# Attention on one core: VectorE empties the second pair of banks, in plain order; and three smaller moves

## The chip, the cores and the metric

The kernel runs on 1 core of one Trainium2 chip. The metric is device time in microseconds (us) of one execution; the time given is the median of several runs. Engine names: PE is TensorE (PEld its weight loads), DVE is VectorE, ACT is ScalarE, POOL is GpSimd, SP is SyncE, which here only issues DMAs.

## What is computed

Four images x of 64 x 64 positions and 256 channels, a self-attention block with a residual:

```python
B, W, H, C = x.shape          # 4, 64, 64, 256
N = W * H                     # 4096
q = jnp.einsum('bwhc,cd->bwhd', x, Wq) + bq      # C2 = 128 channels
k = jnp.einsum('bwhc,cd->bwhd', x, Wk) + bk
v = jnp.einsum('bwhc,cd->bwhd', x, Wv) + bv      # 256 channels
pq = q.reshape(B, -1, N); pk = k.reshape(B, -1, N); pv = v.reshape(B, -1, N)
energy = jnp.einsum('bcn,bcm->bnm', pq, pk)
attention = jax.nn.softmax(energy, axis=-1)
out = jnp.einsum('bcm,bnm->bcn', pv, attention)
return gamma * out.reshape(B, W, H, C) + x
```

All is float32.

## The kernel before

**Products in three parts.** PE multiplies in a reduced form of float32, so every operand is split into a high part h, a low part l and a combination d, and a product is the sum of three: h with h, l with l, d with d, scaled. Each 128x1024 tile that enters a product so costs one ScalarE pass for h (`upper`, L380) and two VectorE passes for l and d (`halves`, L405 and L407).

**Image 0** is projected first, in 16 units i (NI = 16). A unit transposes a piece of x, splits it (`x_forms`: ScalarE h, VectorE l, POOL d), multiplies it with the weights for q and k together (`products(..., 0, ...)`) and for v (`products(..., 1, ...)`), and splits the results again: `qk_forms` into a tile `f`, from which `store` sends k to DRAM (kf) and q to DRAM (qd) with SP's queue; `v_forms` straight into `vall`. Three tiles `f` take turns. In units 0 to 13 POOL makes the d of v, in the last two VectorE makes both (L164). The PSUM banks of these products come from two rings: the transposes take p0 and p1 in turn (ring 0), the q/k and v products a0, b0, a1, b1 in turn (ring 1). Between the units stand the loads of q (`load_q(0, 0, j)`, a quarter at units 1 to 4), the loads of k (`load_k`, units 2, 4, 6, 8, 11), all on POOL's queue, and the first attention work: `cross` and `energy` of steps 0 and 1, `upper` and `halves(0)`.

**Attention** is 512 steps n, 128 to an image. Eight groups of 16 steps (t = 0 to 15, NU = 16) to an image; a group is 512 query positions, a step 256 key positions. In step n the program does, in this order:

- `cross(n + 2)`: two products d of the energy, each in its own bank, then ScalarE scales the bank in place (L357).
- `attend(n, 0)`: six products of the exponentials with v, for the first 128 output channels; h and l go to bank a0, d to b0, summed over the 16 steps of the group.
- `energy(n + 2)`: four more products into the energy banks, then ScalarE's exponential (L374).
- `upper(n + 2)`: ScalarE's h of them; at t = 0 also `upper(n + 1)`, put off from the step before.
- `step(p, ...)`: a piece of the projection of the next image, spread over the steps.
- `halves(n + 1)`: VectorE adds the exponentials to the running sum (L391), then l (L405) and d (L407).
- `attend(n, 1)`: the same six products for the other 128 channels, banks a1 and b1.

All is written in program order, and each engine takes its instructions in that order; no scheduler changes it.

**At a group's end** the four banks are emptied into a tile `o` by `emptied`, scaled by gam2 and gam1: ScalarE, a pass of 128x512 for each bank (L442). a0 and b0 at t = 15; a1 and b1 in the first step of the next group (images 0 to 2, after `energy`), or in its step t = 1 (image 3, which the code calls `late`). In image 3 the second pair of every other group lies in p0 and p1 instead of a1 and b1, so there the emptying is not urgent. In images 0 to 2 it is: `attend(n, 1)` of t = 0 writes the same banks. The program therefore puts products of the next step in front of it, and takes them out of that step:

```python
            if t == 1 and n > 1 and not late:
                attend(n, 0, (2,))
...
            if t == 0 and n and not late:
                attend(n + 1, 0, (0, 1))
            attend(n, 1)
```

`sums` then adds up the softmax sums on PE (z, L466), and `finish` divides, adds x and stores, in pieces over the following steps.

Of the kernel before, what the change touches and what calls it, by code (L numbers as in the profile page):

```python
# [9 lines left out]
F32 = mybir.dt.float32  # L10
F32R = mybir.dt.float32r
I32 = mybir.dt.int32
AF = mybir.ActivationFunctionType
ALU = mybir.AluOpType
# [6 lines left out]
def kernel(  # L21
# [36 lines left out]
    nc = tc.nc  # L58
    B, W, H, C = x.shape
    P = 128  # L60
# [4 lines left out]
    NI = NM // 2  # L65
# [17 lines left out]
    NJ = NB // P  # L83
    NG = N // NB
# [16 lines left out]
    with ExitStack() as fast:  # L101
# [85 lines left out]
        def bank(name, shape, b, ring):  # L187
            if b:
                tile_ = spare(name, shape)
                now["turn"] += 1  # L190
                return tile_
            pool, tag = next(rings[ring])
            return pool.tile(shape, F32, tag=tag, name=name)
# [45 lines left out]
        def products(b, i, w, fs):  # L239

            xf = units["xf", b, i]
            if fs[0] == 2:
                units[w, b, i] = bank(f"qv{w}_{b}_{i}", [P, 2, C], b, 1)
            to = units[w, b, i]
            for s in range(2):
                for f in fs:
                    for k in range(KC):
                        if w:
                            left, right = wf[:, 1, f, k, s * P : (s + 1) * P], xf[f][:, k]
                        else:  # L250
                            left, right = xf[f][:, k, s, :], wf[:, 0, f, k]
                        nc.tensor.matmul(  # L252
                            to[:, s, :],
                            left,
                            right.rearrange("p s a -> p (s a)") if w else right,
                            start=(f == 2 and s == k == 0),
                            stop=(f == 1 and k == KC - 1),
                            skip_group_check=True,
                        )
# [35 lines left out]
        def qk_forms(b, i):  # L295
            y = units.pop((0, b, i)).rearrange("p s (w a) -> p s w a", w=2)
            if b == 0 and i % 3 == 2:
                f = f3
            else:
                f = work.tile([P, 2, 2, 3, P], F32R, tag="pf", name=f"f_{b}_{i}")  # L300
            h = f[:, :, :, 0, :]
            nc.scalar.activation(h, y, AF.Identity, scale=UPPER / 64)  # L302
            yield
            for j, s, op in ((1, -64.0, ALU.add), (2, 64.0 * (1.0 + E), ALU.subtract)):
                nc.vector.scalar_tensor_tensor(  # L305
                    f[:, :, :, j, :], h.bitcast(F32), s, y, ALU.mult, op
                )
                yield
            for s in range(2):
                stores.append((kf[b, i // 2 + NU // 2 * s][:, i % 2], f[:, s, 1]))  # L310
                stores.append((qd[b, i // NJ + NG // 2 * s][:, i % NJ], f[:, s, 0]))

        def v_forms(i):
            y = units.pop((1, 0, i))
# [9 lines left out]

        def store():
            for to, f in stores:
                nc.sync.dma_start(to, f.bitcast(F32))
            stores.clear()

        def load_v(b, t):  # L330
            for i in range(2):
                nc.gpsimd.dma_start(vall[:, t, i], vf[b, t][:, i])

        def load_q(b, g, j=None):
            loads["q", b, g] = qs[g % 2]
            j = slice(NJ) if j is None else j
            nc.gpsimd.dma_start(loads["q", b, g][:, j], qd[b, g][:, j])

        def load_k(n):
            b, u = divmod(n, STEPS)  # L340
            if b < B:
                t = kpool.tile([P, 2, 3, P], F32R, tag="k", name=f"k_{b}_{u}")
                nc.gpsimd.dma_start(t, kf[b, u % NU])  # L343
                loads["k", n] = t
# [89 lines left out]
                        skip_group_check=True,  # L434
                    )

        def emptied(n, j, banks=None):

            if j == 0:
                now["o"] = work.tile([P, 2, 2, NB], F32, tag="o", name=f"o_{n // NU}", bufs=1)  # L440
            for c, scale in enumerate((gam2, gam1)):
                nc.scalar.activation(  # L442
                    now["o"][:, c, j, :],
                    banks[c] if banks else now["ab"[c], j],
                    AF.Identity,
                    scale=scale,
                )

        def sum_forms(n):

# [163 lines left out]
        rings = cycle(now["banks"]), cycle([(ps_o, tag) for tag in ("a0", "b0", "a1", "b1")])  # L614
        image(0)
        qs = [work.tile([P, NJ, 3, P], F32R, tag=f"q{g}", name=f"q{g}", bufs=1) for g in range(2)]
        f3 = qs[1].rearrange("p (s w) f a -> p s w f a", s=2)
        for i in range(4):
            load_x(0, i)
# [27 lines left out]
        for i in range(NI):  # L647
            products(0, i, 0, (0, 1))
            qk = qk_forms(0, i)
            next(qk)  # L650
            if i == 0:
                products(0, 0, 1, (2,))
                seed_v(0)
                transposed(0, 2)
                load_x(0, 5)
                x2 = x_forms(0, 2)
                next(x2)
                next(x2)
            if i + 1 < NI:
                products(0, i + 1, 0, (2,))  # L660
                seed_qk(0, i + 1)
            next(qk)
            next(qk)
            next(qk, None)
            products(0, i, 1, (0, 1))
            vs = v_forms(i)
            next(vs)
            next(vs)
            next(vs, None)
            if i + 1 < NI:  # L670
                products(0, i + 1, 1, (2,))
                seed_v(i + 1)
            if i + 3 < NI:
                transposed(0, i + 3)
                for _ in x_forms(0, i + 3):
                    pass
            load_x(0, i + 6)
            store()
            if i in (7, 10):
                cross(i // 9)  # L680
            elif i in (8, 11):
                energy(i // 9)
            elif i in (9, 12):
                upper(i // 10)
            elif i == 14:
                halves(0)
            if 1 <= i <= NJ:
                load_q(0, 0, i - 1)
            if i in (2, 4, 6):
                load_k(i // 2 - 1)  # L690
            elif i in (8, 11):
                load_k(3 + i // 9)
        for n in range(B * STEPS):
            b, u = divmod(n, STEPS)
            g, t = divmod(u, NU)
            final = n == B * STEPS - 1
            if n == 0:
                image(1)
                load_x(1, 0)
            if u == STEPS - 5 and b + 2 < B:  # L700
                image(b + 2)
            if n == B * STEPS - 6:
                xr = ppool.tile([P, 2, NB], F32, tag="s", name="xr")
                nc.sync.dma_start(xr, xg[b, g])
            cross(n + LOOK)
            turn = t == NU - 1 and not final
            if t == 0 and n:
                upper(n + LOOK - 1)
            if turn:
                zf = sum_forms(n)  # L710
                next(zf)
            p = n - 3 + (n > 6) + (n > 17)
            step(p, "act")
            late = n >= (B - 1) * STEPS
            if t == 1 and n > 1 and not late:
                attend(n, 0, (2,))
            elif not final:
                attend(n, 0)
            energy(n + LOOK)
            load_k(n + LOOK + 3)  # L720
            store()
            if t == 0 and n:
                done = full
            if t == late and n > 1:
                emptied(n - 1 - late, 1, done)
            if turn:
                emptied(n, 0)
            else:
                upper(n + LOOK)
            step(p, "pe")  # L730
            if t == 2 * late and n > 2:
                sums(n - 1 - 2 * late)
                active.append(finish(n // NU - 1, now["o"], now["total"]))
            halves(n + 1)
            if turn:
                next(zf)
            step(p, "dve")
            if final:
                finish_last(n, xr)
                break  # L740
            if t == 0 and n and not late:
                attend(n + 1, 0, (0, 1))
            attend(n, 1)
            full = now["a", 1], now["b", 1]
            if n in (6, 17):
                for engine in ("act", "pe", "dve"):
                    step(p + 1, engine)
            if t == 6 and n + NU < B * STEPS:
                load_q(*divmod(n // NU + 1, NG))
            if n >= STEPS - NU + 3 and (n - 3) // NU % NG == NG - 1 and (n - 3) // STEPS + 1 < B:  # L750
                load_v((n - 3) // STEPS + 1, (n - 3) % NU)
            proceed()

    NB = 512
    NG = N // NB
# [214 lines left out]
```

## Time and profile before

| | us |
|---|---|
| median of 3 runs | 2358.7 (2357.61 to 2360.9) |
| profiled execution | 2356.93 |
| its span, first to last instruction | 2354.9 |
| PE busy | 2340.9 (99%) |
| VectorE busy | 2126.2 (90%) |
| ScalarE busy | 1852.4 (79%) |
| POOL busy | 416.8 (18%) |

The granted TensorE clock is 0.999 of full speed over the span. The profiled execution is 1.8 us shorter than the median of the runs. In the rows of a timeline the first number is the start in us from the span's beginning, the second how long the row lasts; rows of several instructions are merged (x4). The end of a matmul is modelled, and matmuls overlap, so from one start to the next is what counts. The bracket at the end of a row is the idle time of the engine ahead of it and what ended it. In a list of waits the columns are: engine, what waited, what it waited for, us in total, how many times, the longest.

### The profile page before, as it was taken

What the parts mean: (1) busy time and instruction counts of PE and PEld (TensorE: products, weight loads), DVE (VectorE), ACT (ScalarE), POOL (GpSimd) and SP (SyncE); (2) the same over time, 40 slices, a digit from 0 to 9 for tenths busy, and PEclk for the clock granted to TensorE, in tenths of its full rate; (3) what the DMA queues carried; (4) which work ended last, traced back from release to release, by engine and by line L of the source; (5) the groups of instructions that cost most, each with busy time, mean ns of one, the idle gap of its engine ahead of it and who ended that gap; (6) DMA issues with size and microseconds to landing.
All of it is one profiled execution on the core that took longest, in us unless ns stands there. A gap on an engine that the chain in (4) does not pass through costs nothing.

```text
span 2354.9 us, 31737 instructions
## 1 busy us (share of the span) xinstructions
PE 2340.9 (99%) x10820; PEld 1937.3 (82%) x10820; DVE 2126.2 (90%) x2098; ACT 1852.4 (79%) x3026; POOL 416.8 (18%) x716
## 2 busy tenths in 40 slices
PE   9999999999999999999999999999999999999998
PEld 9888888888888888888888888888888888888887
DVE  7998999999999989999899998999989888888888
ACT  7778777787777877778777788777887777788875
POOL 7111111111321111111131111111113111111110
PEclk9999999999999999999999999999999999999999
DMA  8555665566974666545697555655569644444443
GB/s 284 152 171 164 183 172 150 155 171 182 295 243 149 177 175 172 163 145 169 182 323 229 142 178 168 186 158 150 167 178 339 172 134 123 123 130 112 133 133 96
DMA packets 192650, 413.68 MB, mean 176 GB/s; under 512 B 27585, under 2 KB 78019, under 8 KB 192482
## 3 DMA queue, kind: packets, MB, share of 16 engines
q0 software_dynamic: 101120, 280.54, 44.0%
q1 hardware_dynamic: 90814, 130.77, 15.9%
q8 instruction: 89, 1.46, 0.3%
q14 instruction: 79, 0.65, 0.1%
q10 hardware_dynamic: 548, 0.26, 0.0%
HBM read 306.51 MB, written 104.98 MB: 175 GB/s over the span
## 4 chain that ended last, share of the span: by engine, by line
PE 95%; ACT 2%; DVE 1%; issue 1%; POOL 1%; DMA 0%; DVEq 0%; POOLq 0%; ACTq 0%
PE a L428 39%; PE e L371 20%; PE b L428 19%; PE e L356 10%; PE qv L252 4%; PE v L269 3%; PE xt L218 1%; ACT o L442 1%; ACT x L374 1%; PE z L466 1%; ACT e L357 0%; DMA xs<-in_x_dram 0%; DVE ld L405 0%; ACT h L380 0%; POOL v L160 0%
## 5 line engine op out<-in xcount | busy, mean ns | idle before, releaser
L374 ACT ACTIVATE x<-e 128x512 f32<-128x512 f32 x960 | 522.0, 596 | 299.7 <-PE e L371 299.6
L405 DVE TENSOR_TENSOR ld<-x,h 128x1024 fp32r<-128x1024 f32 x480 | 585.9, 1221 | 94.0 <-ACT h L380 48.7
L391 DVE TENSOR_TENSOR s<-s,x 128x1024 f32<-128x1024 f32 x480 | 586.2, 1221 | 87.1 <-ACT x L374 84.5
L357 ACT ACTIVATE e<-e 128x512 f32<-128x512 f32 x1024 | 547.1, 573 | 138.1 <-PE e L356 138.1
L428 PE MATMUL a<-ld,v 128*128 128x512 f32 x2048 | 634.1, 391 | 1.0
L428 PE MATMUL a<-h,v 128*128 128x512 f32 x2048 | 634.2, 391 | 0.0
L428 PE MATMUL b<-ld,v 128*128 128x512 f32 x2048 | 631.2, 389 | 0.6 <-DVE ld L407 0.5
L343 POOL DMA_DIRECT2D k<-kf x512 | 272.4, 532 | 1890.4 <-PE e L371 1754.9
L407 DVE SCALAR_TENSOR_TENSOR ld<-h,x 128x1024 fp32r<-128x1024 f32 x480 | 584.7, 1218 | 0.0
L371 PE MATMUL e<-q,k 128*128 128x512 f32 x2048 | 552.3, 391 | 1.1
L380 ACT ACTIVATE h<-x 128x1024 fp32r<-128x1024 f32 x480 | 511.0, 1065 | 13.2
L371 PEld LDWEIGHTS e<-q,k 128*128 128x128 f32 x2048 | 379.4, 188 | 94.8 <-ACT e L357 19.9
L428 PEld LDWEIGHTS a<-ld,v 128*128 128x128 f32 x2048 | 382.5, 188 | 90.2 <-DVE ld L405 11.1
L428 PEld LDWEIGHTS b<-ld,v 128*128 128x128 f32 x2048 | 384.1, 188 | 82.3 <-issue 1.1
L428 PEld LDWEIGHTS a<-h,v 128*128 128x128 f32 x2048 | 379.6, 188 | 75.1
L356 PE MATMUL e<-q,k 128*128 128x512 f32 x1024 | 315.6, 389 | 0.0
L356 PEld LDWEIGHTS e<-q,k 128*128 128x128 f32 x1024 | 191.9, 188 | 40.2
L305 DVE SCALAR_TENSOR_TENSOR f<-f,qv 128x512 fp32r<-128x512 f32 x118 | 79.2, 679 | 2.5 <-ACT f L302 2.2
L252 PE MATMUL qv<-wf,xf 128*128 128x256 f32 x576 | 77.5, 285 | 1.7 <-POOL xf L160 1.2
L252 PEld LDWEIGHTS qv<-wf,xf 128*128 128x128 f32 x576 | 73.8, 191 | 5.0 <-POOL xf L160 1.8
L164 DVE SCALAR_TENSOR_TENSOR vf<-vf,v 128x512 fp32r<-128x512 f32 x96 | 65.3, 680 | 0.0
L405 DVE TENSOR_TENSOR ld<-s,h 128x1024 fp32r<-128x1024 f32 x32 | 39.2, 1226 | 28.7 <-ACT h L380 27.3
(91 smaller groups left out, 1163.5 us busy)
## 6 DMA issues: line engine op xcount, KB each, us to landing
k<-kf POOLq DMA_DIRECT2D x512, 384.0 KB, 3.4
vf<-vf SPq DMA_DIRECT2D x96, 384.0 KB
v<-vf POOLq DMA_DIRECT2D x96, 384.0 KB, 6.6
q<-qd POOLq DMA_DIRECT2D x31, 768.0 KB, 4.9
kf<-f SPq DMA_DIRECT2D x118, 192.0 KB
qd<-f SPq DMA_DIRECT2D x118, 192.0 KB
o<-in_x_dram POOLq DMA_DIRECT2D x31, 512.0 KB, 7.0
out_dram<-o SPq DMA_DIRECT2D x31, 512.0 KB
```

The lines of the kernel that those rows point to most:

```text
L252: nc.tensor.matmul(to[:, s, :], left, right.rearrange("p s a -> p (s a)") if w else right, start=(f == 2 and s == k == 0), stop=(f == 1 an ...
L305: nc.vector.scalar_tensor_tensor(f[:, :, :, j, :], h.bitcast(F32), s, y, ALU.mult, op)
L343: nc.gpsimd.dma_start(t, kf[b, u % NU])
L356: nc.tensor.matmul(e, *forms(n, i, 2), start=True, stop=False, skip_group_check=True)
L357: nc.scalar.mul(e, e, -REST)
L371: nc.tensor.matmul(e, *forms(n, i, f), start=False, stop=(f == 1), skip_group_check=True)
L374: nc.scalar.activation(x[:, i, :], e, AF.Exp, scale=(1.0 + E) ** 3 / E)
L380: nc.scalar.activation(h, units[n], AF.Identity, scale=UPPER)
L391: nc.vector.tensor_tensor(s, s, x, ALU.add)
L405: nc.vector.tensor_tensor(l, x, h.bitcast(F32), ALU.subtract)
L407: nc.vector.scalar_tensor_tensor(d, h.bitcast(F32), 1.0 + E, x, ALU.mult, ALU.subtract)
L428: nc.tensor.matmul(to, vall[:, t, i, f, j * P : (j + 1) * P], units[n][f][:, i, :], start=(t == 0 and i == 0 and f != 1), stop=(t == NU - ...
```

## The change

Four edits:

- **Second pair by VectorE.** In images 0 to 2 the banks a1 and b1 are emptied by VectorE (`tensor_scalar`), at t = 0 after the projection's piece for PE and `sums`, ahead of `halves(n + 1)`. The order of the attention products is plain again: `attend(n, 0)` whole in every step, nothing pulled ahead.
- **Last image.** ScalarE empties one bank of the second pair at t = 1 and one at t = 2, each ahead of `energy`.
- **First q copied in SBUF.** The four quarters of the first group's q go from `f` straight to the SBUF tile of q, with POOL's queue, and are not stored to DRAM and loaded again. The loads of k stand at units 3, 6, 9, 11, 13.
- **Last v forms put off.** In units 14 and 15 the v products lie in p0 and p1 instead of b0 and b1, and VectorE's l and d of them come later: those of unit 14 after the q/k forms of unit 15, those of unit 15 after `halves(1)` in step 0.

```diff
             if fs[0] == 2:
-                units[w, b, i] = bank(f"qv{w}_{b}_{i}", [P, 2, C], b, 1)
+                ring = 1
+                if b == 0 and w and i >= NI - 2:
+                    ring = 0
+                    next(rings[1])
+                units[w, b, i] = bank(f"qv{w}_{b}_{i}", [P, 2, C], b, ring)
...
                 stores.append((kf[b, i // 2 + NU // 2 * s][:, i % 2], f[:, s, 1]))
-                stores.append((qd[b, i // NJ + NG // 2 * s][:, i % NJ], f[:, s, 0]))
+                if b or s or i >= NJ:
+                    stores.append((qd[b, i // NJ + NG // 2 * s][:, i % NJ], f[:, s, 0]))
+                else:
+                    stores.append((loads["q", 0, 0][:, i], f[:, s, 0]))
...
             for to, f in stores:
-                nc.sync.dma_start(to, f.bitcast(F32))
+                if to.dtype == F32R:
+                    nc.gpsimd.dma_start(to, f)
+                else:
+                    nc.sync.dma_start(to, f.bitcast(F32))
...
-        def emptied(n, j, banks=None):
+        def emptied(n, j, banks=None, only=None, vector=False):
...
             for c, scale in enumerate((gam2, gam1)):
-                nc.scalar.activation(
-                    now["o"][:, c, j, :],
-                    banks[c] if banks else now["ab"[c], j],
-                    AF.Identity,
-                    scale=scale,
-                )
+                if only in (None, c):
+                    y = banks[c] if banks else now["ab"[c], j]
+                    to = now["o"][:, c, j, :]
+                    if vector:
+                        nc.vector.tensor_scalar(to, y, scale, None, ALU.mult)
+                    else:
+                        nc.scalar.activation(to, y, AF.Identity, scale=scale)
...
             next(qk, None)
+            if i == NI - 1:
+                next(vs)
+                next(vs, None)
             products(0, i, 1, (0, 1))
             vs = v_forms(i)
             next(vs)
-            next(vs)
-            next(vs, None)
+            if i < NI - 2:
+                next(vs)
+                next(vs, None)
...
-            if 1 <= i <= NJ:
-                load_q(0, 0, i - 1)
-            if i in (2, 4, 6):
-                load_k(i // 2 - 1)
-            elif i in (8, 11):
-                load_k(3 + i // 9)
+            if i in (3, 6, 9):
+                load_k(i // 3 - 1)
+            elif i in (11, 13):
+                load_k(i // 2 - 2)
...
-            if t == 1 and n > 1 and not late:
-                attend(n, 0, (2,))
-            elif not final:
+            if not final:
                 attend(n, 0)
+            if late and 1 <= t <= 2 and n > 1:
+                emptied(n - 1 - t, 1, done, t - 1)
             energy(n + LOOK)
...
-            if t == late and n > 1:
-                emptied(n - 1 - late, 1, done)
...
+            if t == 0 and n and not late:
+                emptied(n - 1, 1, done, vector=True)
             halves(n + 1)
+            if n == 0:
+                next(vs)
+                next(vs, None)
...
-            if t == 0 and n and not late:
-                attend(n + 1, 0, (0, 1))
             attend(n, 1)
```

More of the change, by code (lines that the diff above doesn't have):

```diff
@@ L332, in load_v, with load_q @@
                 nc.gpsimd.dma_start(vall[:, t, i], vf[b, t][:, i])
-        def load_q(b, g, j=None):
+        def load_q(b, g):
             loads["q", b, g] = qs[g % 2]
-            j = slice(NJ) if j is None else j
-            nc.gpsimd.dma_start(loads["q", b, g][:, j], qd[b, g][:, j])
+            nc.gpsimd.dma_start(loads["q", b, g], qd[b, g])
         def load_k(n):
@@ L616 @@
         qs = [work.tile([P, NJ, 3, P], F32R, tag=f"q{g}", name=f"q{g}", bufs=1) for g in range(2)]
+        loads["q", 0, 0] = qs[0]
         f3 = qs[1].rearrange("p (s w) f a -> p s w f a", s=2)
```

## Prediction

> **What bounds the kernel now.** I read the page first, then the waits of the weight loads, then the timeline of one group boundary engine by engine. The page says that TensorE (PE) has no room:
>
> ```profile
> span 2354.9 us, 31737 instructions
> ## 1 busy us (share of the span) xinstructions
> PE 2340.9 (99%) x10820; PEld 1937.3 (82%) x10820; DVE 2126.2 (90%) x2098; ACT 1852.4 (79%) x3026; POOL 416.8 (18%) x716
> ```
>
> By the matmul row the most that any reordering can win is 2354.9 - 2340.9 = 14.0 us. But matmul ends are modelled, so a matmul that starts late is hidden under the stretched end of the one before. The weight loads show it:
>
> ```profile
> PEld e L371 <- ACT e L357: 19.9, 62, 0.6
> PEld a L428 <- DVE ld L405: 11.1, 23, 0.5
> PEld qv L252 <- POOL xf L160: 1.8, 2, 1.4
> ```
>
> [...]
>
> The counts give the places away. 23 is the number of group boundaries whose new group lies in the first three images (24 groups, less the start). 62 is twice 31, that is 23 and the 8 boundaries of the last image. So two waits come back at each boundary of images 0 to 2 and one at each of image 3. One such boundary (step 160 has t = 0, step 161 t = 1), on PE:
>
> ```profile
> 798.97 0.63 PE L428 MATMUL a<-h,v 128*128 128x512 f32 x2
> 799.65 0.73 PE L428 MATMUL a<-ld,v 128*128 128x512 f32 x2
> 800.22 0.62 PE L428 MATMUL a<-h,v 128*128 128x512 f32 x2
> 800.68 0.62 PE L428 MATMUL a<-ld,v 128*128 128x512 f32 x2
> 801.14 0.62 PE L428 MATMUL b<-ld,v 128*128 128x512 f32 x2
> 801.59 0.61 PE L356 MATMUL e<-q,k 128*128 128x512 f32 x2
> 802.05 0.61 PE L428 MATMUL b<-ld,v 128*128 128x512 f32 x2
> 802.65 1.22 PE L371 MATMUL e<-q,k 128*128 128x512 f32 x4
> 803.71 1.03 PE L218 MATMUL xt<-ident,x 128*128 128x128 f32 x8
> ```
>
> Starts are what counts. An undisturbed pair takes 0.46 us (800.22 to 801.14 is two pairs). The first two rows are the pulled-forward products `attend(161, 0, (0, 1))`: from h to l takes 0.68, and l itself 0.57, so 0.22 + 0.11 = 0.33 us are lost on l(161), VectorE's L405. The pair left over for t = 1 (802.05) takes 0.60 and the four energy products 1.06 instead of 0.92: 0.14 + 0.14 = 0.28 us lost, on ScalarE's pass L357 over the energy bank, because only two products stand between `cross` and `energy`. Together 0.61 us a boundary.
>
> **Part 1: second pair emptied by VectorE, plain order.** Both places where PE waits come from the order that the change removes. Is there room for two more VectorE passes? VectorE and ScalarE at the same boundary:
>
> ```profile
> 795.16 0.68 DVE L164 SCALAR_TENSOR_TENSOR vf<-vf,v 128x512 fp32r<-128x512 f32 x1
> 795.76 1.22 DVE L391 TENSOR_TENSOR s<-s,x 128x1024 f32<-128x1024 f32 x1
> 798.37 1.22 DVE L405 TENSOR_TENSOR ld<-x,h 128x1024 fp32r<-128x1024 f32 x1 [1.39 <-ACT h L380]
> 799.51 1.22 DVE L407 SCALAR_TENSOR_TENSOR ld<-h,x 128x1024 fp32r<-128x1024 f32 x1
> ```
>
> ```profile
> 796.26 1.10 ACT L357 ACTIVATE e<-e 128x512 f32<-128x512 f32 x2
> ...
> 799.20 0.69 ACT L442 ACTIVATE o<-a,gam 128x512 f32<-128x512 f32 x1
> 799.77 0.70 ACT L442 ACTIVATE o<-b,gam 128x512 f32<-128x512 f32 x1
> 800.34 1.08 ACT L380 ACTIVATE h<-x 128x1024 fp32r<-128x1024 f32 x1
> 801.29 0.56 ACT L467 COPY s<-z 1x512 f32<-1x512 f32 x1
> 802.02 1.07 ACT L357 ACTIVATE e<-e 128x512 f32<-128x512 f32 x2 [0.17 <-PE e L356]
> ```
>
> The trace has no VectorE pass that reads only PSUM. The nearest is L305, one full bank and one SBUF operand:
>
> ```profile
> L305 DVE SCALAR_TENSOR_TENSOR f<-f,qv 128x512 fp32r<-128x512 f32 x118 | 79.2, 679 | 2.5 <-ACT f L302 2.2
> ```
>
> Rows of that size start 0.60 us apart (795.16 to 795.76), so I take 1.2 us for the pair; ScalarE's own 0.70 each, 1.4 us, is the upper bound, and the lower one is nothing, if it were to fit wholly into idle time. [...]
>
> In the new order VectorE reaches the two passes at 795.84 (795.16 + 0.68). The banks were filled before PE went on to the energy bank that ScalarE starts on at 796.26, so the passes begin between 795.9 and 796.3 and end between 797.1 and 797.7. Queued behind them on VectorE are the running sum L391 (pitch 1.14), then l, then d. The sum ends at 798.2 to 798.8 and l can start where it does now (798.37, held by h) or 0.4 later: the 1.39 us in which VectorE waits for h is what hides the passes. d is then done between 800.73 (799.51 + 1.22) and 801.15. Who waits for it: PE. With z done at 798.97, plain order gives `attend(160, 1)` to 800.35, `cross(163)` to 800.81, h and l of `attend(161, 0)` to 801.73, and only then d. It is 0.6 to 1.0 us early; l has still more. Without the cover the pair's whole 1.2 us would come on top and PE would lose 0.2 to 0.6 us there.
>
> The other side of the same step: ScalarE loses 799.20 to 800.34, 1.14 us, so h(162) runs 799.20 to 800.28 and the copy of z to about 800.8. `cross(163)` now starts at 800.35; today its ScalarE pass starts 0.43 after it (801.59 to 802.02), so it starts at about 0.8, ends for the first half at 801.35 and wholly at 801.9. `energy(163)` comes at 800.81 + 6 x 0.23 = 802.19. No wait is left, with 0.3 us to spare on the second half and 0.8 on the first. `attend(160, 1)` at 798.97 writes banks that were emptied by 797.7. VectorE's later steps carry the same work as now, and the steps after t = 1 have no wait on it in the list above. So both losses go: 23 x 0.61 = 14.0 us, bounds 0 and 14.0 for a wait that comes back elsewhere.
>
> **Part 2: last image, one bank per unit.** The step pair t = 1, 2 of its first boundary:
>
> ```profile
> 1826.82 0.61 PE L428 MATMUL b<-ld,v 128*128 128x512 f32 x2
> 1827.57 1.20 PE L371 MATMUL e<-q,k 128*128 128x512 f32 x4
> 1828.61 0.63 PE L466 MATMUL z<-q,ones 128*128 128x512 f32 x2
> ```
>
> ```profile
> 1823.84 1.09 ACT L374 ACTIVATE x<-e 128x512 f32<-128x512 f32 x2 [0.93 <-PE e L371]
> ...
> 1826.90 1.10 ACT L357 ACTIVATE e<-e 128x512 f32<-128x512 f32 x2
> ```
>
> 0.75 - 0.46 and 1.04 - 0.92 make 0.41 us lost on L357, late because both evictions ran at t = 1. In the change the first pass (0.69) goes ahead of `energy`, into the 0.93 us in which ScalarE is idle before 1823.84, and costs nothing; the second goes to t = 2, again ahead of the exponentials. L357 of t = 2 then starts about 0.95 us earlier, well before 1827.27. The second pass pushes the exponentials of t = 2 by 0.2 us at most, and z reads the emptied bank after it. 8 x 0.41 = 3.3 us, bounds 0 and 3.3.
>
> **Part 3: first image.** q copied in SBUF, k loads later. POOL and PE at the one long stop:
>
> ```profile
> 28.96 1.30 POOL L160 TENSOR_TENSOR xf<-xf 128x512 fp32r<-128x512 f32 x1
> 31.85 0.56 POOL L337 DMA_DIRECT2D q<-qd  x1 [1.59 <-DMA qd<-f]
> ...
> 34.21 1.27 POOL L160 TENSOR_TENSOR xf<-xf 128x512 fp32r<-128x512 f32 x1
> ```
>
> ```profile
> 33.12 1.20 PE L252 MATMUL qv<-wf,xf 128*128 128x256 f32 x8
> 35.53 0.74 PE L252 MATMUL qv<-wf,xf 128*128 128x256 f32 x4 [1.22 <-POOL xf L160]
> ```
>
> POOL stands 1.59 us until a store of q has landed, with `x_forms` queued behind it, and PE then waits 1.22 us. The copy needs only VectorE's finished forms, so this wait goes; POOL still issues four DMAs, each one unit earlier, and SP four fewer. Against that the copies are issued behind POOL's own products, later than SP stored q, and they hold the `f` buffer that ScalarE's next forms reuse: up to four waits, none longer than the 1.59 that a landing costs here, 6.4 us at worst. I take a gain of 0.9, bounds +1.2 and -5.2.
>
> **Part 4: last v forms put off.** Two VectorE passes of image 0 go behind the forms of step 0, two behind those of step 1, and v's last units leave PE's attention banks alone. PE's waits there go at first, but VectorE is the bound in those steps:
>
> ```profile
> 70.00:80.00 10.00, 9.90 (x43) 7.72 (x42) 9.90 (x10) 7.59 (x13) 1.42 (x3) 1.00 0.73 207
> ```
>
> VectorE is busy 9.90 of 10 us and the work is only moved, so what PE wins at steps 0 and 1 it mostly waits at steps 2 and 3. I take 0.3 us; bounds 0 and 1.0.
>
> Sum: 14.0 + 3.3 + 0.9 + 0.3 = 18.5 us. The profiled execution took 2356.93 us, so 2338.4 for it; the median of the runs stands 1.8 above that execution, which gives **2340.2 us**.
>
> **Rivals.** (A) *The waits move.* VectorE is late with d(161), or the plain order finds another pass late, and about half of part 1 comes back: 7 us less, 2347 us. For it: margins of 0.3 to 1.0 us in a step where VectorE has just taken 1.2 us more. Against: the idle 1.39 us stands at the right place. (B) *VectorE becomes the bound, and slower.* If the passes cannot use that idle time and the group stays VectorE-bound to its end, each group pays the 1.2 us and gains nothing: 23 x 1.2 = 27.6 more, less 3.3 and 1.2 of the other parts, 2382 us. It decides when the pair takes longer than idle, margin and saving together, 1.39 + 1.0 + 0.61 = 3.0 us, against 1.2 to 1.4 by the rows; or when VectorE idles nowhere else in a group, and it is busy only 90%. (C) *The change doesn't do what it says:* the copies' landings hold ScalarE in the first image, part 3 costs up to 5.2 us instead of gaining 0.9: up to 2346 us.
>
> **Chances.** Forecast 0.74, its own range 2336 to 2344; A 0.12; C 0.06; B and other losses 0.08. About 0.2% (4.7 us) is what a measurement of this kernel can tell from no change. The forecast, A and C all lie below 2354: faster 0.90. Slower, from B, 0.07; 0.03 is left for halves of B that just cancel the gain. The range takes in the forecast's own and A: 2336 to 2348.
>
> **What would show it.** After: the row "PEld a L428 <- DVE ld L405" gone from 23 and "PEld e L371 <- ACT e L357" down from 62 to a few; two VectorE rows of 0.6 to 0.7 us between L164 and L391 at each boundary and the 1.39 us idle before L405 nearly gone; in the last image no gap ahead of L371 at t = 2; POOL without the 1.59 us at unit 4; boundaries 72.36 instead of 72.97 us apart. Wrong: a new PEld wait on L407 with count 23, an idle PE before `attend(n, 1)`, or ScalarE's L302 waiting on the copies in the first 35 us.

## The result and the profile after

The changed kernel takes 2338.23 us (median of 6 runs, 2337.45 to 2340.22), the kernel before 2358.88 us beside it (6 runs): a ratio of 0.9913, 95% interval 0.99 to 0.9926. The profiled execution took 2337.63 us, its span 2335.8 us. The forecast was 2340.2 us.

The page of the changed kernel, busy times:

```profile
span 2335.8 us, 31727 instructions
## 1 busy us (share of the span) xinstructions
PE 2325.0 (100%) x10820; PEld 1944.9 (83%) x10820; DVE 2151.9 (92%) x2144; ACT 1829.1 (78%) x2980; POOL 416.2 (18%) x716
```

VectorE has 46 instructions more and ScalarE 46 fewer: 23 boundaries, two banks. The matmul row shows 10.8 us of room now and 14.0 before, a difference of 3.2 us, where the span fell by 19.1. The waits of the weight loads, changed kernel, the first three:

```profile
PEld b L437 <- DVE ld L416: 2.0, 4, 0.8
PEld wp L139 <- DVE ones L131: 1.1, 1, 1.1
PEld xt L218 <- issue: 0.8, 1, 0.8
```

The wait on l (23 times) and the wait on ScalarE's pass over the energy bank (62 times) are gone from the list altogether. What leads it now are four waits on d. Two of them, 1.42 us, lie in steps 2 and 3 of image 0 (below), one of 0.17 in step 1, and one of 0.42 in the last step of all, where the kernel before had it too.

The same boundary as in the prediction, steps 160 and 161, on VectorE of the changed kernel (L455 is the new pass, L400 the sum, L414 l, L416 d):

```profile
788.40 0.68 DVE L164 SCALAR_TENSOR_TENSOR vf<-vf,v 128x512 fp32r<-128x512 f32 x1
789.00 0.75 DVE L455 TENSOR_SCALAR o<-a,gam 128x512 f32<-128x512 f32 x1
789.66 0.74 DVE L455 TENSOR_SCALAR o<-b,gam 128x512 f32<-128x512 f32 x1
790.32 1.22 DVE L400 TENSOR_TENSOR s<-s,x 128x1024 f32<-128x1024 f32 x1
791.61 1.23 DVE L414 TENSOR_TENSOR ld<-x,h 128x1024 fp32r<-128x1024 f32 x1
792.75 1.22 DVE L416 SCALAR_TENSOR_TENSOR ld<-h,x 128x1024 fp32r<-128x1024 f32 x1
```

and on PE, from `attend(160, 1)` on (L365 is `cross`, L380 `energy`):

```profile
792.21 0.63 PE L437 MATMUL a<-h,v 128*128 128x512 f32 x2
792.68 0.62 PE L437 MATMUL a<-ld,v 128*128 128x512 f32 x2
793.14 0.63 PE L437 MATMUL b<-ld,v 128*128 128x512 f32 x2
793.61 0.62 PE L365 MATMUL e<-q,k 128*128 128x512 f32 x2
794.07 0.62 PE L437 MATMUL a<-h,v 128*128 128x512 f32 x2
794.52 0.62 PE L437 MATMUL a<-ld,v 128*128 128x512 f32 x2
794.98 0.61 PE L437 MATMUL b<-ld,v 128*128 128x512 f32 x2
795.43 1.07 PE L380 MATMUL e<-q,k 128*128 128x512 f32 x4
796.34 1.03 PE L218 MATMUL xt<-ident,x 128*128 128x128 f32 x8
```

Every pair starts 0.45 to 0.47 us after the one before. The 1.39 us in which VectorE waited for h are filled. d(161) is done at 793.97 and PE wants it at 794.98.

Where the time went, by stages, from the starts of the cross products in the two traces (us):

| | first q/k product to cross(0) | cross(0) to step 0 | step 0 to 4 | 4 to 16 | 16 to 384 | 384 to 509 | to the end |
|---|---|---|---|---|---|---|---|
| before | 31.38 | 27.85 | 18.50 | 54.60 | 1678.33 | 517.38 | 20.22 |
| after | 29.92 | 27.78 | 18.48 | 54.62 | 1663.98 | 514.27 | 19.71 |

The difference is 14.35 us at the 23 boundaries, 3.11 in the last image, 1.5 in the first image's projection and 0.02 in steps 0 to 4; another 0.07 lies between cross(0) and step 0, which no part aims at. The 0.44 us that the changed kernel starts its first product later and the 0.51 at the end belong to no edit.

### The profile page after: what moved, and what is told of

Same layout as the page of the kernel before. It is cut to its first block, busy times and chain, and to the rows that moved or that the text cites. A ratio compares the mean times of both kernels' runs of the same rounds, so it can differ in the third digit from the quotient of the medians.

```text
span 2335.8 us, 31727 instructions
## 1 busy us (share of the span) xinstructions
PE 2325.0 (100%) x10820; PEld 1944.9 (83%) x10820; DVE 2151.9 (92%) x2144; ACT 1829.1 (78%) x2980; POOL 416.2 (18%) x716
## 4 chain that ended last, share of the span: by engine, by line
PE 99%; DVE 1%; DMA 0%; issue 0%; ACT 0%; DVEq 0%
PE a L437 40%; PE b L437 20%; PE e L380 20%; PE e L365 10%; PE qv L256 5%; PE v L273 3%; PE xt L218 1%; PE z L476 1%; DMA xs<-in_x_dram 0%; DVE ld L414 0%; DVE ld L416 0%; DVE v L164 0%; DVE f L309 0%; DVE q L309 0%; DVE s L400 0%
## 5 line engine op out<-in xcount | busy, mean ns | idle before, releaser
L400 DVE TENSOR_TENSOR s<-s,x 128x1024 f32<-128x1024 f32 x480 | 587.1, 1223 | 78.5 <-ACT x L383 76.3
L414 DVE TENSOR_TENSOR ld<-x,h 128x1024 fp32r<-128x1024 f32 x480 | 586.7, 1222 | 58.7 <-PE b L437 40.8
L416 DVE SCALAR_TENSOR_TENSOR ld<-h,x 128x1024 fp32r<-128x1024 f32 x480 | 585.8, 1220 | 0.0
L380 PE MATMUL e<-q,k 128*128 128x512 f32 x2048 | 548.2, 390 | 0.0
L380 PEld LDWEIGHTS e<-q,k 128*128 128x128 f32 x2048 | 384.5, 188 | 79.5
L365 PE MATMUL e<-q,k 128*128 128x512 f32 x1024 | 316.1, 390 | 0.0
L365 PEld LDWEIGHTS e<-q,k 128*128 128x128 f32 x1024 | 192.0, 188 | 40.1
L309 DVE SCALAR_TENSOR_TENSOR f<-f,qv 128x512 fp32r<-128x512 f32 x118 | 79.5, 681 | 0.3
L164 DVE SCALAR_TENSOR_TENSOR vf<-vf,v 128x512 fp32r<-128x512 f32 x96 | 65.4, 682 | 0.6 <-ACT vf L154 0.6
L414 DVE TENSOR_TENSOR ld<-s,h 128x1024 fp32r<-128x1024 f32 x32 | 39.2, 1226 | 28.7 <-ACT h L389 27.2
```

The lines of the kernel that those rows point to most:

```text
L309: nc.vector.scalar_tensor_tensor(f[:, :, :, j, :], h.bitcast(F32), s, y, ALU.mult, op)
L365: nc.tensor.matmul(e, *forms(n, i, 2), start=True, stop=False, skip_group_check=True)
L380: nc.tensor.matmul(e, *forms(n, i, f), start=False, stop=(f == 1), skip_group_check=True)
L400: nc.vector.tensor_tensor(s, s, x, ALU.add)
L414: nc.vector.tensor_tensor(l, x, h.bitcast(F32), ALU.subtract)
L416: nc.vector.scalar_tensor_tensor(d, h.bitcast(F32), 1.0 + E, x, ALU.mult, ALU.subtract)
```

## Experiments

**Engine and order, each alone.** Three kernels, each the changed one with one part of edit 1 undone.

Plain order, but ScalarE empties:

```diff
             if t == 0 and n:
                 done = full
+            if t == 0 and n and not late:
+                emptied(n - 1, 1, done)
...
-            if t == 0 and n and not late:
-                emptied(n - 1, 1, done, vector=True)
```

> Plain order as in the changed kernel, but ScalarE empties a1 and b1, at its old place after energy. Theory (order and engine are needed together): ScalarE frees a1 only about 0.9 us after PE wants to write it (799.20 + 0.69 against 798.97 in the old trace), so each of the 23 boundaries loses about 1.05 us in a wait of PE or PEld on ScalarE's eviction ahead of attend(n, 1): 2338.2 + 24 = 2362 us, slower than the old kernel. Rival (the order alone brings the gain): no such wait, 2338 us.

Measured: 2362.35 us (9 runs), against 2357.01 for the kernel before beside it, ratio 1.0024 (1.0013 to 1.0034). Steps 16 to 384 take 1688.41 us, 24.4 more than in the changed kernel, 1.06 us a boundary. PE and PEld in that kernel at one boundary:

```profile
803.30 0.63 PE L476 MATMUL z<-q,ones 128*128 128x512 f32 x2
804.75 0.73 PE L437 MATMUL a<-h,v 128*128 128x512 f32 x2 [0.82 <-ACT o L457]
805.33 0.62 PE L437 MATMUL a<-ld,v 128*128 128x512 f32 x2
```

```profile
PEld a L437 <- ACT o L457: 29.0, 23, 1.3
```

PE stands before the bank that ScalarE has yet to empty. Plain order with ScalarE at its old place, behind the exponentials, is slower than the old kernel. ScalarE at that boundary:

```profile
803.04 1.09 ACT L383 ACTIVATE x<-e 128x512 f32<-128x512 f32 x2
804.01 0.69 ACT L457 ACTIVATE o<-a,gam 128x512 f32<-128x512 f32 x1
```

ScalarE's passes ahead of the exponentials, the place that part 2 gives them in the last image, were not run at these boundaries. By these rows the first would then start at 803.04 and be done at about 803.73, when PE asks for a1 (0.46 after 803.30), with the exponentials 1.14 us later. So these runs show that the banks have to be free earlier; whether ScalarE could have done that too, and at what price, stays open.

VectorE empties, old order:

```diff
-            if not final:
+            if t == 1 and n > 1 and not late:
+                attend(n, 0, (2,))
+            elif not final:
                 attend(n, 0)
...
+            if t == 0 and n and not late:
+                attend(n + 1, 0, (0, 1))
             attend(n, 1)
```

> VectorE empties a1 and b1 as in the changed kernel, but with the old order of the products (two thirds of the next step's first half pulled ahead). Theory (the losses come from the order): l of the next step is still held by h, and the energy products still follow their cross products too closely, so both old losses of 0.33 and 0.28 us come back at each of 23 boundaries: 2338.2 + 14 = 2352 us. Rival (ScalarE's two passes were the cause, whatever the order): 2338 us.

Measured: 2352.58 us (10 runs), ratio to before 0.9983 (0.9974 to 0.9993). Steps 16 to 384: 1678.64 us, the old figure. Both old waits are back, under the new line numbers:

```profile
PEld e L380 <- ACT e L366: 14.0, 46, 0.4
PEld a L437 <- DVE ld L414: 11.2, 23, 0.5
```

Both undone (the two edits above together):

> All of part 1 undone (ScalarE empties the second pair, old order), parts 2 to 4 kept. Theory: 23 x 0.62 = 14.3 us come back, 2352.5 us, with the old waits of PEld on L405-type l (23 times) and on the energy pass. Rival (a good share of the gain came from parts 2 to 4): under 2347 us.

Measured: 2352.05 us (10 runs), ratio 0.998 (0.997 to 0.999); steps 16 to 384: 1678.57 us, with the same two rows. So with the old order it makes no difference which engine empties the banks (0.07 us over 23 boundaries). The old order loses 0.63 us a boundary by itself, and the plain one needs the banks free earlier, as VectorE's passes make them. Parts 2 to 4, which this kernel keeps, are worth 4.96 us in its median (95% interval 2.4 to 7.1) and 4.6 by the table of stages.

**How deep is the cover?** Each VectorE pass run twice:

```diff
             if t == 0 and n and not late:
                 emptied(n - 1, 1, done, vector=True)
+                emptied(n - 1, 1, done, vector=True)
```

> Each VectorE pass over a1 and b1 is run twice, so a boundary has 1.32 us more VectorE work ahead of the running sum. Theory (the passes cost nothing because VectorE had to wait for h there, and that cover is now used up: l starts 0.07 us after the sum ends, d is 1.0 us early): d is now late by 0.32 us, with the restart of PE some 0.4 to 0.5 us a boundary, 23 times a wait of PEld on d: 2338.2 + 10 = 2348 us. Rival (VectorE, 92% busy, has room anyway): 2338 us. Rival (VectorE is the bound through the group): 23 x 1.32 = 30 us more, 2368 us.

Measured: 2346.51 us (4 runs), ratio 0.9958 (0.9941 to 0.9974). Steps 16 to 384 take 8.66 us more than in the changed kernel, 0.38 a boundary. VectorE and PE there:

```profile
794.97 1.22 DVE L400 TENSOR_TENSOR s<-s,x 128x1024 f32<-128x1024 f32 x1
796.10 1.22 DVE L414 TENSOR_TENSOR ld<-x,h 128x1024 fp32r<-128x1024 f32 x1
797.24 1.22 DVE L416 SCALAR_TENSOR_TENSOR ld<-h,x 128x1024 fp32r<-128x1024 f32 x1
```

```profile
797.85 0.61 PE L437 MATMUL a<-ld,v 128*128 128x512 f32 x2
798.51 0.73 PE L437 MATMUL b<-ld,v 128*128 128x512 f32 x2
799.08 1.09 PE L380 MATMUL e<-q,k 128*128 128x512 f32 x4
```

d ends at 798.46 and the pair starts at 798.51, 0.66 after the one before instead of 0.46; the next start is 0.57 behind it, 0.11 late as well. That is 0.31 of the 0.38; the other 0.07 these rows do not show. Of 1.32 us more work 0.94 vanish and 0.38 come out as time: the cover is the 1.0 us by which d was early, neither nothing nor endless. In the changed kernel VectorE is 92% busy, and PE's weight loads wait for d 4 times in all (2.0 us); with the passes run twice it is 27 times (12.7 us), 23 of them more, one a boundary.

**Last image: place or halving?** Both passes at t = 1, but ahead of `energy`:

```diff
-            if late and 1 <= t <= 2 and n > 1:
-                emptied(n - 1 - t, 1, done, t - 1)
+            if late and t == 1 and n > 1:
+                emptied(n - 1 - t, 1, done)
```

> Last image: ScalarE empties both banks of the second pair at t = 1, but ahead of energy as in the changed kernel (it did so behind it before). Theory (the place ahead of energy, in ScalarE's idle 0.93 us, is what counts; halving only helps): ScalarE's exponentials of t = 1 come 0.3 to 0.4 us later, its pass over the energy bank of t = 2 still ends before PE's products, so at most 0.05 us a boundary is lost, 0.4 us in all. Rival (one bank per unit is what counts): 0.4 us a boundary, 3 us in all, with a wait of PEld on that pass 8 or 16 times.

Measured (one run): steps 384 to 509 take 514.27 us, the same as in the changed kernel to the hundredth. ScalarE in that kernel, t = 1:

```profile
1808.25 0.68 ACT L457 ACTIVATE o<-a,gam 128x512 f32<-128x512 f32 x1
1808.83 0.69 ACT L457 ACTIVATE o<-b,gam 128x512 f32<-128x512 f32 x1
1809.39 1.09 ACT L383 ACTIVATE x<-e 128x512 f32<-128x512 f32 x2
```

The second pass eats the rest of the idle time and a little more, and no wait of PE follows. The place did it; one bank per unit was not needed. Halving without the new place was not run.

**First image.** Part 3 undone, whole and by halves: q's quarters loaded from DRAM again, the k loads at their old units, or both.

```diff
-            if i in (3, 6, 9):
-                load_k(i // 3 - 1)
-            elif i in (11, 13):
-                load_k(i // 2 - 2)
+            if 1 <= i <= NJ:
+                load_q(0, 0, i - 1)
+            if i in (2, 4, 6):
+                load_k(i // 2 - 1)
+            elif i in (8, 11):
+                load_k(3 + i // 9)
```

> All of part 3 undone: q's first quarters go to DRAM and are loaded, k loads at units 2, 4, 6, 8, 11. Theory: POOL's wait for a landing store comes back around unit 4 or 5 and PE waits 1.2 to 1.5 us for x_forms; the span from PE's first 256-column product to the first cross product grows by 1.5 us. Rival (the wait had another cause, and part 3 is worth under 0.3 us): no difference.

> q's first quarters go to DRAM and are loaded again as before; the k loads stay at their new units. Theory (the load of q, issued one unit after its store, is what POOL stands on): POOL waits for a landing store of q again and PE for x_forms, 1 to 2.7 us more up to the first cross product than in the changed kernel. Rival (the early k loads were the cause): within 0.3 us of it.

> Only the times of the k loads are undone, q is still copied in SBUF. Theory (the wait was on the store of q): as the changed kernel within 0.3 us. Rival (POOL's wait is on any store that has just been issued, k's too): half or more of the 1.5 us comes back, in a wait of POOL on a k load.

Measured (one run each), first q/k product to cross(0): both undone 32.65 us, q loaded alone 31.58, k early alone 30.93; changed kernel 29.92. Where q is loaded PE stands at one spot each time, but not the same one. Both undone, POOL:

```profile
33.47 0.56 POOL L344 DMA_DIRECT2D q<-qd  x1 [2.86 <-DMA qd<-f]
34.03 0.54 POOL L350 DMA_DIRECT2D k<-kf  x1
```

POOL waits 2.86 us for the store of q to land, and PE's weight loads 2.7 us for `x_forms` behind it. With q alone loaded POOL does not wait at all (contrary to what was expected); PE does, at cross(0), for the load itself:

```profile
36.42 0.60 PE L218 MATMUL xt<-ident,xs 128*128 128x128 f32 x4
38.44 0.71 PE L363 MATMUL e<-q,k 128*128 128x512 f32 x2 [1.41 <-DMA q<-qd]
```

With k early alone neither of the two things that were expected came: 1.0 us more than in the changed kernel, and no wait of POOL. Here the copies hold something up. ScalarE and PE there:

```profile
33.29 0.60 ACT L306 ACTIVATE f<-qv 128x512 fp32r<-128x512 f32 x1 [1.94 <-PE qv L256]
```

```profile
35.35 0.71 PE L256 MATMUL qv<-wf,xf 128*128 128x256 f32 x4 [0.79 <-DVE f L309]
```

The products that the first row names were done long before; what ends the wait is the copy out of the `f` buffer that L306 writes. POOL issued it at 27.39, with a k load issued at 24.34 ahead of it, and it took 5.8 us to land. VectorE's L309 and then PE follow. In the changed kernel POOL issued the same copy at 27.42, ahead of its first k load, and it took 3.2 us. The same pass of ScalarE there (unit 6), and with it that of unit 3, which writes the buffer of unit 0:

```profile
22.23 0.60 ACT L306 ACTIVATE f<-qv 128x512 fp32r<-128x512 f32 x1 [0.49 <-PE qv L256]
...
31.62 0.60 ACT L306 ACTIVATE f<-qv 128x512 fp32r<-128x512 f32 x1
```

Unit 6 does not wait. Unit 3 waits 0.49 us; here too the products were done, and the copy of the first quarter, issued at 17.80, landed 4.3 us later, just before 22.23. PE does not notice: neither PE nor its weight loads have a row in the list of waits from 16 to 37 us, and the kernel with all of part 1 undone has no wait at unit 3 and takes 29.91 us. Nine traces run the same program in this stretch (all those with part 3 whole). Six take 29.70 to 29.92 us; the other three, two of 30.80 and one of 31.47, have a stretch of slow matmuls at the start (last section), which the four traces with something undone do not have. Against the mean of the six the halves cost 1.7 us (q loaded) and 1.1 (k early), and 2.8 both together. These are single runs, and the kernel before, with the same two things undone, takes 31.38 where this one takes 32.65: POOL's wait there was 1.59 us, here 2.86. So that both halves do something is shown by the named waits; how much each is worth is known to about a microsecond.

**Last v forms.** Part 4 undone:

```diff
-            if i == NI - 1:
-                next(vs)
-                next(vs, None)
             products(0, i, 1, (0, 1))
...
-            if i < NI - 2:
-                next(vs)
-                next(vs, None)
+            next(vs)
+            next(vs, None)
...
-            if n == 0:
-                next(vs)
-                next(vs, None)
```

(and the banks from ring 1 as before).

> Part 4 undone: last v forms at their old place and in the old banks. Theory (VectorE is the bound from unit 14 to step 3, and the put-off passes only moved the waits): the cross product of step 4 comes as long after that of step 0 as in the changed kernel, within 0.2 us (18.5 us); PE waits at steps 0 and 1 again instead of 2 and 3. Rival: 1 us longer.

Measured (one run): step 0 to step 4 takes 18.54 us, 18.48 in the changed kernel, 18.50 in the kernel before. Part 4 is worth nothing as it stands: VectorE works without a gap there (9.90 of the 10 us from 70 to 80 in the changed kernel and in the one before) and its work is the same. PE in the changed kernel, steps 2 and 3:

```profile
73.92 0.61 PE L437 MATMUL a<-ld,v 128*128 128x512 f32 x2
74.77 0.72 PE L437 MATMUL b<-ld,v 128*128 128x512 f32 x2 [0.23 <-DVE ld L416]
...
78.55 0.61 PE L437 MATMUL a<-ld,v 128*128 128x512 f32 x2
79.50 0.73 PE L437 MATMUL b<-ld,v 128*128 128x512 f32 x2 [0.34 <-DVE ld L416]
```

Two ways to take work off VectorE there were tried. First, POOL makes the d of the last two v units:

```diff
-            yield from split(*(vall[:, i, :, f] for f in range(3)), y, i < NI - 2)
+            yield from split(*(vall[:, i, :, f] for f in range(3)), y, True)
```

> The changed kernel, but POOL makes the d of the last two v units as it does for the others: VectorE has two passes of 0.6 us less between unit 14 and step 3. Theory (VectorE is the bound there): the waits of 0.50 and 0.61 us at steps 2 and 3 go, step 0 to step 4 takes 17.4 instead of 18.5 us, 2337.1 us in all, which timing can hardly tell and the trace can. Rival (PE is then held by h, by the energy pass or by POOL): no gain, a wait of another name at steps 1 to 3.

Measured: 2338.28 us (5 runs), ratio to before 0.9921 (0.9907 to 0.9935); step 0 to step 4 takes 19.47 us, one us *more*. That is neither of the two things expected: the wait is still on d. VectorE and POOL:

```profile
66.94 1.22 DVE L414 TENSOR_TENSOR ld<-x,h 128x1024 fp32r<-128x1024 f32 x1
68.07 2.32 DVE L416 SCALAR_TENSOR_TENSOR ld<-h,x 128x1024 fp32r<-128x1024 f32 x1
```

```profile
67.18 2.14 POOL L160 TENSOR_TENSOR v<-v 128x512 fp32r<-128x512 f32 x1 [4.51 <-DMA kf<-q]
```

VectorE's d takes 2.32 us instead of 1.22, and POOL's pass 2.14 instead of 1.29, when they overlap. The two passes that POOL took over save VectorE 1.2 us and cost it 2.2.

Second, VectorE's work is only put in another order: v's last unit after `halves(2)`, the sum of step 3 behind its l and d.

```diff
-            if n not in (1, 2):
+            if n not in (1, 2, 3):
                 summed()
...
-            if n in (1, 2):
+            if n in (1, 2, 3):
                 summed()
...
-            if n == 0:
+            if n == 1:
                 next(vs)
                 next(vs, None)
```

> The changed kernel, with VectorE's work of the first steps in another order: l and d of v's last unit come after halves(2) instead of halves(1), and the running sum of step 3 behind its l and d. Theory (VectorE is the bound in steps 1 to 3 and has 1.8 us to spare from step 4): d(2) and d(3) come 1.2 and 1.1 us earlier, the waits of 0.50 and 0.61 us go, step 0 to step 4 takes 17.4 instead of 18.5 us; 2337.1 us in all. Rival (the waits move to step 4 or 5, or the late v forms hold the bank that the next image's transposes want): no gain.

Measured: step 0 to step 4 takes 17.30 us, 1.18 less. PE at the same two places (both without a wait):

```profile
75.39 0.62 PE L437 MATMUL a<-ld,v 128*128 128x512 f32 x2
75.84 0.62 PE L437 MATMUL b<-ld,v 128*128 128x512 f32 x2
...
79.47 0.62 PE L437 MATMUL a<-ld,v 128*128 128x512 f32 x2
79.92 0.62 PE L437 MATMUL b<-ld,v 128*128 128x512 f32 x2
```

In all 2336.96 us (5 runs), ratio to before 0.9913 (0.99 to 0.9927): the lowest median of this study, but within the interval of the changed kernel, so only the trace shows the gain.

## Why the prediction was right, and where its terms were off

- **The reading.** That PE's 99% hid the loss, that the weight loads' waits count it, and that the starts size it (0.61 us a boundary) held: 14.35 / 23 = 0.62. The busy share of the weight loads moved only from 82% to 83%: their list of waits sized the loss, their share did not.
- **Part 1** (14.0, which was also its upper bound; measured 14.35). Two of its sizes were off, in opposite directions. The pass over a bank took 0.74 to 0.75 us, starts 0.66 apart, not 0.60; the pair costs 1.32 us, between the 1.2 that was taken and the upper bound of 1.4. In return it started at once behind L164 (789.00), where the prediction allowed up to 0.4 us for the banks to fill. d was 1.0 us early, the upper end of the stated 0.6 to 1.0, and running the passes twice found that margin again. That margin is why neither size mattered, and rival A would have needed it to be gone. Rival B put its turning point at 3.0 us for the pair; with 2.64 us steps 16 to 384 still took 5.69 us less than in the kernel before, so the turning point does lie beyond that.
- **The hardest step of part 1**, that order and engine go only together, was implied by the prediction and is shown by the three kernels above, for ScalarE at its old place: 1688.41, 1678.64 and 1678.57 us against 1663.98.
- **Part 2** (3.3, measured 3.11). Right, for the first reason given: the pass goes into ScalarE's idle time ahead of the exponentials. The second, one bank per unit, was not needed.
- **Part 3** (0.9, at most 1.2; measured 1.5 between the two traces). The wait named is gone. The upper bound was too low: it was PE's idle time in the matmul row (1.22), the row that part 1 had found to hide waits, while the weight loads' own waits on POOL's pass came to 1.8. Rival C, the copies holding ScalarE's next forms, shows at 0.49 us in the changed kernel, where it costs PE nothing, and at 1.94 us, more than the 1.59 allowed for one such wait, where the k loads stay early: the later k loads, which the prediction gave no price of their own, belong to the cover. The two traces with q loaded and k early differ by 1.3 us among themselves, so the term cannot be sized better than that.
- **Part 4** (0.3, measured 0.02). The mechanism was named rightly, waits moving from steps 0 and 1 to 2 and 3. The term should have been nothing: with VectorE 9.90 of 10 us busy and no work removed, nothing can be won before its first gap.
- **The sum** was 18.5; it is 19.1 in the traces and 20.65 in the medians. Part 3 came out 0.6 above its term and part 4 0.3 below, so it is partly luck that the sum is nearer than they are. The profiled execution before (2356.93) lies below all six runs of that kernel. The forecast took its distance of 1.8 us from the median over to the changed kernel, where it is 0.6: of the 2.0 us between forecast and median, 1.2 come from that.

## What to carry to other kernels

Before calling an engine full, look at starts and at the waits of its weight loads; at a busy share of 99% the matmul row showed 14.0 us of room here, and 19.1 were won. The products pulled forward to cover a late buffer cost 0.63 us a boundary here, where the wait itself, in plain order with ScalarE at its old place, cost 1.06: they had to be ready themselves (the wait on l, 11.2 us in 23 boundaries) and were missing where they were taken from (the wait on the energy pass, 14.0 us, 46 times). So free the buffer earlier with an engine that is waiting for something else at that moment, and check how far the next thing on that engine is early: here that idle time (1.39 us) and that margin (1.0) hid a pair of passes of 1.32 us whole, and 0.94 of the 1.32 of a second pair. Where VectorE had no gap, moving its work within the stretch won nothing (0.02 us); moving it past the next slack won 1.18.

## What was not expected of the hardware

In the kernel where POOL makes the d of the last two v units, POOL and VectorE held each other up where both worked from SBUF: VectorE's two-operand pass took 2.32 instead of 1.22 us and POOL's 2.14 instead of 1.29. In the projection of image 0 the same POOL passes (1.28 to 1.34 us) run beside VectorE passes with one operand in PSUM, 0.68 to 0.70 us each, and neither grows. POOL's pass starts at 67.18 under a VectorE pass that ends at 68.16, after its usual 1.22 us, and the next VectorE pass ends 1.1 us late. The second pass that POOL took over shows the same: it starts at 72.22 and takes 2.21 us, and VectorE's d from 73.19 on takes 2.32. What causes it was not tried.

A VectorE pass that scales one bank of PSUM by a factor for each partition (gam) took 0.74 to 0.75 us, longer than one that reads a bank and an SBUF tile (0.68), and longer than ScalarE's 0.68 to 0.70 for the same work. The two VectorE passes also differ in the operation and in the type they write; which of these makes the difference was not tried.

TensorE's granted clock was halved for some 3 us near the start in two of the nine executions that run the same program there; in one of them it was 0.85, 0.50 and 0.79 in the three windows of 2 us from 6 to 12. Windows of the kernel with both passes ahead of `energy`, then of the changed kernel (stretch, length, busy time of PE, PEld, DVE, ACT and POOL, granted clock, DMA share, GB/s):

```profile
8.00:10.00 2.00, 2.00 (x11) 2.00 (x10) 1.69 (x3) 0.70 (x2) 0.68 (x4) 0.50 0.20 70
```

```profile
8.00:10.00 2.00, 1.60 (x14) 1.40 (x13) 2.00 (x5) 0.60 (x1) 0.69 (x4) 1.00 0.35 104
```

At 0.50 PE is busy throughout with fewer products: the eight of 128x256 that start at 9.01 take 1.84 us to the start of the next (10.85), where the changed kernel takes 1.06 (8.89 to 9.95). This execution is one of the two that take 30.80 us in the first image; the other shows 0.50 from 10 to 12 us. The kernel with plain order on ScalarE (31.47 us) takes 1.85 us for the same eight (9.77 to 11.62) and 0.85 for the next four, 213 ns each, where the changed kernel takes 0.48, 120 ns each. The windows view gives 1.00 for the clock there, so a lower clock is not shown for that run. What sets the slow stretch off was not tried.
